# Two more expert blocks in seven-product form, and the last block's slot scatters issued together

## The chip, the cores and the metric

The kernel runs on one core of a Trainium2 chip. The metric is the device time of one execution in microseconds (us); the time before is the median of ten runs. All arithmetic is float32.

## The reference, cut to what matters

One causal self-attention layer over 4096 rows of 256, with a residual, and then a mixture of experts with a residual. The second half is where the change lies:

```python
h = layernorm(x) @ W_in + b_in                       # 4096 tokens x 256
probs = softmax(h @ W_gate + b_gate)                 # 8 experts
topv, topi = top_k(probs, 2); topv /= topv.sum()     # each token goes to two experts
mid  = relu(einsum('nd,edh->neh', h, W1) + b1)       # 256 -> 1024
eout = einsum('neh,ehd->ned', mid, W2) + b2          # 1024 -> 256
out  = x + einsum('ne,ned->nd', route, eout) @ W_out + b_out
```

The kernel computes only the two chosen experts of each token.

## The kernel before, in words

**Attention and routing.** Rows are worked in eight blocks of 512 tokens. While attention runs over them, each finished block is routed: every token gets a slot in the list of each of its two experts. A slot is written into the DRAM table `slots` by an indirect DMA on GpSimd (POOL), one for each 128 tokens and each of the two choices, so eight for each block. `put_tile` (L472, L473) is one such scatter: a copy of the 128 addresses to integers, and then the DMA. Scatters that are ready wait in the list `puts`; `put_one` takes one from it and pins it to the place where it is called, so that they are spread between other work.

**Items.** The tokens' slots are then worked as a list `work` of items. Items named `a` and `b` are blocks of 256 slots of one expert; `c`, `d` and `e` are smaller ones of one to four experts; `z` comes last and takes the slots that were left out. The first nine entries (0 to 8) are `a` items, entry 9 is the only `e` item, and entries 10 and 11 are `a` items again. For each item an expert's W1 and W2 are loaded (SyncE, SP), the tokens' rows are gathered (L1146, POOL), turned so that features lie on partitions (`rows_todo`: 32x32 transposes on VectorE (DVE), 16 for a pair of items), multiplied by W1 into `mid` (tiles `pm`), multiplied by W2 (`contribute`, tiles `pe`), and scattered to `parts` (L1531, POOL).

**Stages.** The loop `for n, item in enumerate(work)` runs as stages. Stage n computes `mid` of item n+2 and contributes item n. In the usual form `mid` takes 16 products of 128x256, each followed by an activation on ScalarE (ACT).

**Seven products.** Items for which `seven_of` holds take another form, `hidden_seven`: W1 and the tokens are each cut into a 2x2 matrix of blocks, and seven products take the place of eight, for each of four pairs of feature tiles. That makes 28 products of 128x128. It needs:

- `key_forms` (L1409 to L1412), at the end of stage n for item n+4: four sums of W1's quarters, 128x512 each, on POOL. One of them overwrites a quarter of W1 in place.
- `row_forms` (L1420 to L1423), inside the contribution of stage n for item n+3: four sums of the turned rows' quarters (tile `t`), 128x128 each, on POOL.
- In `hidden_seven` PE does products 0, 4, 1, then 5, 2, then 6 of all four pairs, with some units of item n's contribution between them. DVE then combines each pair (L1473, L1475), and only after L1475 of a pair may PE add product 3 into the same bank. Up to seven of the 16 units of the contribution lie ahead of those last four products, and nine behind them.

Before, the condition is `AHEAD + 3 < n` with `AHEAD = 3`. So items 7, 8, 11 and thirteen later ones have the form, 16 in all.

**Planning.** The last block's tokens (block 7) are entered in stage 0, and their places are counted in stage 1 by `counting()`, which appends eight scatters to `puts`. In stage 1 `plan_late` picks the slots of item `z`, and in stage 2 `plan` is called four times (tables `b`, `c`, `d`, `e`; L983 to L1020). Both are long chains of very small DVE instructions. From stage 3 on items depend on them: SP first runs `take_late` (L1076, L1077), which reads and clears slots and so waits for all scatters, and then fetches the slots of the `e` item and its successors (L1125) by the tables' addresses. `assert not puts` stands at the beginning of stage 3.

**Order.** Instructions given to `tc.keep_in_program_order` (in the loop by `pin`, from stage 3 on) keep the order in which they are written. The others, the sums of `key_forms`, the transposes of `turn_pair` and the planning among them, are placed by a scheduler when the program is built. After that each engine runs its own list strictly in order, waiting at each instruction for the semaphores of others. `fetch_pair` and `turn_pair` gather and turn two items at a time: 5 and 6, 7 and 8, 9 and 10.

Where the scatters of `puts` are taken in this loop:

```python
            if f % 2:
                put_one(nc.scalar.copy)      # hidden_units: four in each usual mid
...
            pin(nc.vector.tensor_tensor(y[:, u, :], pe[:, :D], c2, ALU.add))
            ease()
            put_one()                        # contribute_units: two in each 256-slot item
```

Of the kernel before, what the change touches and what calls it, by code (L numbers as in the profile page):

```python
# [57 lines left out]
SEVEN = True  # L58
# [5 lines left out]
def preln_attention_moe_kernel(  # L64
# [18 lines left out]
    nc = tc.nc  # L83
# [44 lines left out]
    def ps_o(name):  # L128
        return psum.tile([P, TB], F32, tag="o", name=name, bufs=3)
# [14 lines left out]
    def mul(*a, **k):  # L144
        done = nc.tensor.matmul(*a, **k)  # L145
        if ordered:
            tc.keep_in_program_order(done)
        return done
# [318 lines left out]
    puts = []  # L467
# [18 lines left out]
    def put_one(by=nc.vector.tensor_copy):  # L486

        if puts:
            tc.keep_in_program_order(puts.pop(0)(by=by))
# [592 lines left out]
    AHEAD = 3  # L1082
    FOUR = AHEAD + 6
    ALONE = FOUR + 2
    ALONG = (FOUR + 1,)
# [6 lines left out]
    work, blocks_work = blocks_work[:ALONE], blocks_work[ALONE:]  # L1092
# [300 lines left out]
        return [mid[:, f, :] for f in range(NF)], [partial(finish, f) for f in range(NF)]  # L1393

    def seven_of(n):
        return SEVEN and AHEAD + 3 < n < len(work) and work[n][0] in "ab" and n not in ALONG

    def key_forms(item, got):

# [493 lines left out]
    for n, item in enumerate(work):  # L1893
# [36 lines left out]
        if seven_of(n + 3):  # L1930

            def form(m):
                settle(m - 3.5)
                formed[m].append(row_forms(work[m], hTs[m]))

            forming.append(partial(form, n + 3))
# [6 lines left out]
        if coming + 1 < len(work) and seven_of(coming):  # L1943
            hTs.pop(coming)
            points = pieces + 2
            others = contribute_units(item, got.pop(n), mids.pop(n))
            mids[coming], behind[-coming] = hidden_seven(
                work[coming], got[coming], formed.pop(coming), others, ready
            )
        elif coming + 1 < len(work):  # L1950
            points = pieces + 2
            if "e" in (work[coming][0], work[coming - 1][0]):
                for do in ready:
                    do()
                ready = ()
                contribute(item, got.pop(n), mids.pop(n))
                send_second(upto2[n] + VT)
            mids[coming], behind[coming] = hidden(
                work[coming], got[coming], hTs.pop(coming), ready, False
            )  # L1960
        else:
            points = pieces
            for do in ready:
                do()
# [5 lines left out]
            turn_pair(AHEAD + 2)  # L1970
        if n == 1:
            counting()
        if n == 2:
            pn = ps_o("pnb")
            mul(pn[:, :NE], lhsT=ones, rhs=seen, start=True, stop=True)
            seen = const.tile([P, NE], F32, tag="sums", name="sums")
            nc.vector.tensor_copy(seen, pn[:, :NE])
            tables["b"] = plan("b", seen, NBLK - NFULL, SB, SEI - 1, tables["a"][2])

            def twice(k):  # L1980
                taken = const.tile([P, NE], F32, tag="twice" + k, name="twice" + k)
                nc.vector.tensor_scalar_mul(taken, tables[k][2], 2.0)
                return taken

            tables["c"] = plan("c", seen, NHALF, SH, SEI - 1, twice("b"))
            tables["d"] = plan("d", seen, 2 * NPAIR, SQR, SEI - 1, twice("c"))
            tables["e"] = plan("e", seen, NE, SEI, SEI - 1, twice("d"))
            tables["f"] = tables["e"]

            over = const.tile([P, 1], I32, tag="over", name="over")  # L1990
            nc.vector.tensor_scalar_add(over, tables["d"][3], float(4 - 2 * USUAL))
            nc.vector.tensor_tensor(over, over, tables["e"][3], ALU.max)
# [11 lines left out]
        if seven_of(n + 4):  # L2004
            formed[n + 4] = [key_forms(work[n + 4], got[n + 4])]
# [56 lines left out]
```

## Time and profile before

| | |
|---|---|
| median of ten runs | 1041.98 us (1039.56 to 1042.56) |
| the profiled execution | 1043.04 us |
| its span, first to last instruction | 1041.3 us |
| TensorE (PE) busy | 1032.6 us, 99% |
| DVE, ACT, POOL busy | 706.6, 406.9, 362.0 us |
| mean granted PE clock | 0.998 |
| DMA | 173.59 MB, mean 167 GB/s |

The span is the time between the first and the last instruction; 1.74 us of the execution lie outside it. Times of rows are counted from the span's start. The stages that matter here lie between 572 us (stage 0) and 667 us (the end of stage 6). A matmul of float32 shows as two records, so the 16 products of a usual `mid` are 32 records.

### The profile page before, as it was taken

The numbers are of one execution on the slowest core, as the hardware profiler recorded it, in microseconds if no ns is written. First come the engines' busy times: TensorE is split into PE (matmuls) and PEld (weight loads), VectorE is DVE, ScalarE is ACT, GpSimd is POOL, SyncE is SP. The second block draws the span as 40 slices with busy tenths as digits, with TensorE's granted clock in tenths as the row PEclk, the third lists the DMA queues.
The fourth block names the chain that finished last, engine by engine and source line by source line (L and its number), as shares of the span: only waits on it lengthen the run. The fifth ranks groups of instructions, "written<-read, shape, count | busy, mean of one in ns | idle before, by whom it ended". The sixth has DMA issues, their size and how long they took to land. (4 is left out here: it accounts for less than half of the span.)

```text
span 1041.3 us, 18934 instructions
## 1 busy us (share of the span) xinstructions
PE 1032.6 (99%) x6153; PEld 900.7 (86%) x6153; DVE 706.6 (68%) x2131; ACT 406.9 (39%) x1001; POOL 362.0 (35%) x439
## 2 busy tenths in 40 slices
PE   9999999999999999999999999999999999999998
PEld 7877889989989989999998887888798987889887
DVE  5765668766858777668797683487577675874346
ACT  2442344434425243424333222333443534436254
POOL 2201332212312120222024564354766466457110
PEclk9999999999999999999999999999999999999999
DMA  6433311121121110104455937799999989997685
GB/s 210 135 79 83 78 42 39 49 62 23 42 42 18 46 40 4 44 3 112 113 172 186 329 109 218 234 314 347 353 345 306 312 291 314 325 319 216 210 318 187
DMA packets 194891, 173.59 MB, mean 167 GB/s; under 512 B 82942, under 2 KB 169922, under 8 KB 194788
## 3 DMA queue, kind: packets, MB, share of 16 engines
q1 hardware_dynamic: 185956, 154.36, 47.9%
q0 software_dynamic: 8288, 17.45, 4.9%
q8 instruction: 50, 0.82, 0.3%
q10 hardware_dynamic: 544, 0.52, 0.1%
q14 instruction: 53, 0.43, 0.1%
HBM read 135.15 MB, written 30.44 MB: 159 GB/s over the span
## 5 line engine op out<-in xcount | busy, mean ns | idle before, releaser
L145 PE MATMUL ps<-qT,zT 128*128 128x256 f32 x1088 | 239.9, 373 | 0.8 <-DVE mx L690 0.8
L145 PEld LDWEIGHTS ps<-qT,zT 128*128 128x128 f32 x1088 | 200.8, 190 | 29.3 <-issue 2.2
L145 PE MATMUL po<-v,s 128*128 128x128 f32 (+1 forms) x672 | 125.8, 320 | 0.0
L145 PE MATMUL pe_a<-w_a,mid_a 128*128 128x256 f32 x544 | 124.9, 384 | 0.0
L145 PEld LDWEIGHTS pe_a<-w_a,mid_a 128*128 128x128 f32 x544 | 102.3, 192 | 15.5 <-issue 2.5
L145 PEld LDWEIGHTS po<-v,s 128*128 128x128 f32 x672 | 107.3, 191 | 9.1
L473 POOL DMA_INDIRECT slots<-assign,ati x64 | 63.6, 994 | 147.3 <-DVE ati L472 99.4
L684 ACT COPY s<-ps 128x512 f32<-128x512 f32 x120 | 69.4, 581 | 104.7 <-PE ps L145 99.5
L1292 DVE STREAM_TRANSPOSE hT<-h 32x192 f32<-32x192 f32 x240 | 88.7, 370 | 24.6 <-DMA h<-rows,slot_a 18.0
L787 ACT ACTIVATE s<-s 128x512 f32<-128x512 f32 x120 | 73.0, 629 | 72.7 <-DVE s L784 55.8
L690 DVE TENSOR_TENSOR mx<-ps,mx 128x512 f32<-128x512 f32 x91 | 62.5, 687 | 57.0 <-ACT s L684 56.1
L784 DVE TENSOR_TENSOR s<-s,pmax 128x512 f32<-128x512 f32 x120 | 77.1, 677 | 9.5 <-PE pmax L151 9.3
L145 PE MATMUL po<-v,sf 128*128 128x129 f32 x384 | 74.6, 276 | 0.1
L145 PE MATMUL pm_a<-hT,w_a 128*128 128x256 f32 (+1 forms) x304 | 59.0, 331 | 0.0
L145 PEld LDWEIGHTS po<-v,sf 128*128 128x128 f32 x384 | 58.3, 192 | 0.5 <-DVE sf L823 0.5
L145 PEld LDWEIGHTS pm_a<-hT,w_a 128*128 128x128 f32 x304 | 50.5, 191 | 5.5 <-issue 1.2
L1335 ACT ACTIVATE mid_a<-pm_a,c_a 128x256 f32<-128x256 f32 x64 | 30.3, 474 | 60.4 <-PE pm_a L145 53.7
L145 PE MATMUL pe_b<-w_b,mid_b 128*128 128x256 f32 x224 | 51.7, 380 | 0.1
L1531 POOL DMA_INDIRECT parts<-y_a,slot_a x34 | 34.0, 999 | 50.8 <-DVE y_a L1528 33.8
L1292 DVE STREAM_TRANSPOSE mid_d<-raw_d 32x256 f32<-32x256 f32 x96 | 41.8, 436 | 5.8 <-ACT raw_d L1371 4.3
L145 PEld LDWEIGHTS pe_b<-w_b,mid_b 128*128 128x128 f32 x224 | 41.1, 190 | 5.3 <-issue 0.5
L322 POOL TENSOR_SCALAR ln0rstd<-ln0mv 128x4 f32<-128x4 f32 (+1 forms) x9 | 2.2, 245 | 120.8 <-DVE ln0mv L316 120.2
(388 smaller groups left out, 1997.9 us busy)
## 6 DMA issues: line engine op xcount, KB each, us to landing
w_a<-in_L_ffn_W_dram SPq DMA_DIRECT2D x68, 512.0 KB, 6.1
w_d<-in_L_ffn_W_dram SPq DMA_DIRECT2D x48, 512.0 KB, 7.5
w_c<-in_L_ffn_W_dram SPq DMA_DIRECT2D x32, 512.0 KB, 7.8
w_b<-in_L_ffn_W_dram SPq DMA_DIRECT2D x28, 512.0 KB, 5.6
rows<-hr SPq DMA_DIRECT2D x16, 512.0 KB, 5.0
w_e<-in_L_ffn_W_dram SPq DMA_DIRECT2D x16, 512.0 KB, 5.1
yp<-parts SPq DMA_DIRECT2D x14, 512.0 KB, 7.4
after<-x SPq DMA_DIRECT2D x8, 512.0 KB, 2.9
```

Source lines behind the costliest of these rows:

```text
L145: done = nc.tensor.matmul(*a, **k)
L322: keep(nc.gpsimd.tensor_scalar_add(rstd[:, s, 0], mv[:, s, 1], EPS))
L473: put = nc.gpsimd.indirect_dma_start(out=slots, out_offset=bass.IndirectOffsetOnAxis(ap=ati, axis=0), in_=assign[:, TOPK * (b * TPB + j) + ...
L684: nc.scalar.copy(flat, ps)
L690: done = nc.vector.tensor_tensor(r.mx, ps, old, ALU.max)
L784: nc.vector.tensor_tensor(s, s, pm[:, :QB].unsqueeze(1).to_broadcast([P, KU, QB]), ALU.subtract)
L787: nc.scalar.activation(s, s, AF.Exp)
L1292: pin(easy.pop(0)[1]())
L1335: nc.scalar.activation(mid[f // 2][:, f % 2, :size], pm[:, :size], AF.Relu, bias=c1[:, f : f + 1])
L1531: put = nc.gpsimd.indirect_dma_start(out=parts, out_offset=bass.IndirectOffsetOnAxis(ap=slot[:, u : u + 1], axis=0), in_=y[:, u, :], in_of ...
```

## The change

Two conditions. `seven_of` begins two items earlier, so items 5 and 6 take the form of seven products too: 18 in all. And right after `counting()` in stage 1 all eight scatters of block 7 are issued one behind the other, with their address copies on ACT; before, one copy stood behind each output of items 1 and 2 (on DVE) and one behind every second activation of item 4 (on ACT).

```diff
     def seven_of(n):
-        return SEVEN and AHEAD + 3 < n < len(work) and work[n][0] in "ab" and n not in ALONG
+        return SEVEN and AHEAD + 1 < n < len(work) and work[n][0] in "ab" and n not in ALONG
...
         if n == 1:
             counting()
+            while puts:
+                put_one(nc.scalar.copy)
```

The functions that it calls (`key_forms`, `row_forms`, `hidden_seven`, `put_tile`) are unchanged.

## The prediction

> **What bounds the kernel now.** The page first: PE is busy for 1032.6 of 1041.3 us. Time can therefore only come from fewer products or from PE's own waits.
>
> ```profile
> PE 1032.6 (99%) x6153; PEld 900.7 (86%) x6153; DVE 706.6 (68%) x2131; ACT 406.9 (39%) x1001; POOL 362.0 (35%) x439
> ```
>
> Next, who waited for whom, on PE over the whole span. One entry leads, and it is in the seven-product form: product 3 waits for DVE's second combine.
>
> ```profile
> PE pm_a L145 <- DVE mid_a L1475: 2.1, 4, 1.5
> ```
>
> The timeline of PE (start, length, instruction, records, idle time before it) shows a usual `mid` at 607.30, then item 7's stage (5) up to 653.49, and item 8's.
>
> ```profile
> 607.30 7.07 PE L145 MATMUL pm_a<-hT,w_a 128*128 128x256 f32 x32
> ...
> 641.25 2.76 PE L145 MATMUL pe_a<-w_a,mid_a 128*128 128x256 f32 x12
> 645.51 0.46 PE L145 MATMUL pm_a<-t_a,w_a 128*128 128x128 f32 x2 [1.50 <-DVE mid_a L1475]
> ...
> 647.92 5.74 PE L145 MATMUL pe_a<-w_a,mid_a 128*128 128x256 f32 x18
> 653.49 0.38 PE L145 MATMUL pm_a<-hT,w_a 128*128 128x128 f32 x2
> ...
> 661.87 1.05 PE L145 MATMUL pm_a<-t_a,w_a 128*128 128x128 f32 x8
> ```
>
> Stage 5 lasts from 634.92 to 653.49, 18.57 us. Stage 6, the same work undisturbed, takes 13.13 us. So item 7 loses 5.44 us, more than the 2.1 us of the list of waits. Its four last products take 2.41 us (645.51 to 647.92) and not 0.89, since DVE needs 0.72 for each pair. And the 18 records behind them take 5.57 us where they should take 18 x 0.216 = 3.9. The busy times by stretch say why (last three columns: granted PE clock, DMA share, GB/s): after the gap the clock is half for some 3.5 us.
>
> ```profile
> 644.00:645.50 1.50, 0.01 (x1) 0.02 (x1) 1.33 (x5) 0.00 (x0) 1.20 (x2) 1.00 0.72 218
> ...
> 649.00:650.00 1.00, 1.00 (x4) 0.79 (x3) 0.95 (x3) 0.00 (x0) 0.92 (x4) 0.50 1.01 367
> ...
> 651.50:652.00 0.50, 0.50 (x4) 0.40 (x3) 0.00 (x0) 0.00 (x0) 0.25 (x1) 1.00 1.06 402
> ```
>
> Why DVE was late, from its timeline: it stood 18 us for gathered rows, turned ten tiles of the pair 9/10, and only then came to the combines at 644.54. Before that the planning ran from 604.14 to 620.13, and some of its tiny steps took 1 to 2 us in place of 0.16.
>
> ```profile
> 604.14 0.17 DVE L1977 COPY sums<-pnb 128x8 f32<-128x8 f32 x1
> ...
> 611.45 1.93 DVE L1019 CAST whose_id<-whosed 128x16 int32<-128x16 f32 x1
> ...
> 613.50 1.24 DVE L1982 TENSOR_SCALAR twiced<-nowd 128x8 f32<-128x8 f32 x1
> ...
> 619.96 0.17 DVE L1020 CAST base_ie<-basee 128x8 int32<-128x8 f32 x1
> ...
> 639.76 2.66 DVE L1292 STREAM_TRANSPOSE hT<-h 32x192 f32<-32x192 f32 x7 [18.03 <-DMA h<-rows,slot_a]
> ...
> 644.54 0.29 DVE L1473 TENSOR_TENSOR mid_a<-pm_a,mid_a 128x128 f32<-128x128 f32 x1
> ```
>
> POOL's timeline gives the partner: its four key sums stand at 612.06 to 617.19, and the slow DVE steps end with them. SP's shows where the rows came from: it waited for the last scatter until 620.78.
>
> ```profile
> 577.77 1.00 POOL L1531 DMA_INDIRECT parts<-y_a,slot_a  x1 [0.30 <-issue]
> ...
> 612.06 1.28 POOL L1409 TENSOR_TENSOR s_a<-w_a,w_a 128x512 f32<-128x512 f32 x1
> ...
> 632.78 0.94 POOL L1146 DMA_INDIRECT h<-rows,slot_a  x1 [0.30 <-issue]
> ```
>
> ```profile
> 620.78 0.59 SPq L1076 DMA_DIRECT2D late_slot<-slots  x1
> ...
> 625.23 2.81 SPq L1125 DMA_DIRECT2D slot_e<-slots  x4
> ```
>
> **Part 1, the products.** A usual stage is 13.81 us (607.30 to 621.11), one with seven products 13.13. Two items save 2 x 0.68 = 1.4 us.
>
> **Part 2, the scatters.** The eight still cost 8 x 1.27 = 10.2 us of POOL. In the order of the changed program they stand in one piece ahead of both outputs of item 1, so the last is out near 604 and not at 618.66. SP's wait until 620.78 falls away; its reads by table `e` then start when the planning ends, at P + 0.6, not at 625.23. The eight copies on ACT (0.18 each) lie in its idle time before 594.33. In the changed order three of the ten transposes stand ahead of item 6's combines and the other seven between those and item 7's, a whole stage earlier than needed, so item 7's 5.4 us go.
>
> **Part 3, POOL's queue.** The scheduler put the key sums of items 5 and 6 far ahead: three in front of the second four scatters of block 6, five in front of item 0's output and the four gathers of pair 7/8. Eight times 1.28 is 10.2 us for everything queued behind, the gathers and block 7's scatters. W1 of item 5 is issued at 563.74 and 565.01 and lands 6.5 later (median). So: three sums from 570 to 571.5, four scatters (5.1), the other five sums (6.4), item 0's output (now 577.77) at 585 to 587, gathers until 591 to 593, block 7's scatters and item 1's outputs until 605 to 607, and then the row sums of item 5. PE wants the first of these at 607.5. I take no wait; 1 us at most.
>
> **Part 4, DVE for item 5.** The combines of item 5 stand right behind the planning's last step. Call its end P. The pair 7/8 lands 1 to 3 us later than DVE now takes it (594.81), less the 1.0 us that POOL's key sums cost DVE there: sums start at 604.3 to 606. The planning takes 15.99 us now, 4.6 of which are four steps at 5.23 us in all instead of 0.64. Uncontended from 604.3 it ends at 615.7, and with the row sums of item 5 (four of 0.41 to 0.48) in its way at 616.5. But behind item 2's output, some 4 us before the end, POOL starts the key sums of item 7, the row sums of item 6 and, soon, the rest: about 7 us of sums against a dozen small steps. If these are slowed as now, P is 619 to 621. I take 619.5, near the 620.13 of now.
>
> A DVE instruction with two SBUF inputs, or in a two-port mode, is fully blocked while a GpSimd instruction that reads SBUF runs, says the Trainium skill (SBUF — State Buffer, Who interferes with whom). It speaks against this change, which adds 16 such sums; the 1.93 us row agrees. By it alone, with whoever issues first winning, P could be anything from 616.5 to 621.
>
> PE reaches product 3 of item 5 at 607.30 + 8.38 = 615.7 (8.38 as in stage 6, 653.49 to 661.87). It gets it 0.97 after DVE is free (644.54 to 645.51): 620.5. That is a wait of 4.8, then 1.5 of pacing (2.41 less 0.89), then 1.7 of half clock: 8.0 us. Bounds: P of 616.5 gives 1.8 + 1.5 = 3.3 without a clock drop; P of 621 gives 9.5.
>
> The gate closes after an idle window of about 3.4 us, says the skill (TensorE: Matmul & The Clock Gate, What's actually happening). Here 2.2 us of gaps within 4 us were enough. By the rule the low bound stays 3.3, by the row it would be 5.0; at P = 619.5 both give 8.0.
>
> **Part 5, a new wait for item 6.** In the changed order three transposes of pair 9/10 stand ahead of item 6's combines. Their rows landed at 639.76, 7.0 after the last gather was issued. The gathers now follow item 3's output and POOL's sums: last issue near 628.5 in place of 632.78, landed at 634 to 636; three transposes (0.38 each) and 0.97 make 636 to 638. PE wants it at 607.30 + 13.13 + 8.0 + 8.38 = 636.8. I take 1.2 with some pacing; 0 to 2.7. With a small wait at item 5 it is larger, 2 to 5, as the rows don't come earlier in proportion.
>
> **Sum.** -1.4 - 5.4 + 8.0 + 1.2 = +2.4 us. The profiled execution (1043.04) becomes 1045.4; it lies 1.06 above the median, so the median 1041.98 becomes 1044.4.
>
> **Rivals.** (a) *The wait only moves*, from item 7 to 5 and 6, at the same price: P near 617.5, waits of 5 to 8 together, net -2 to +1.5, about 1042. For it: DVE's steps slip in between POOL's sums, and 0.41 us row sums hold less than 1.28 us ones. (b) *Faster*: the rows of pair 9/10 come with slot reads 5 us earlier and DVE is through its planning by 616, so that PE waits about 1 at item 5 (with pacing 2.5) and 1 at item 6: -6.8 + 3.5 = -3.3, about 1038.7. It decides where P is under 616.5 and the rows land before 631. Against it: the bounds of part 4, and POOL's sums end near 622 whatever DVE does, so that gathers can hardly start before 624. (c) *POOL late as well*: item 5's row sums come after 608.5, which adds a wait on them and pushes all behind: +5, about 1047. That the form isn't taken at all is excluded by the order of the changed program.
>
> **How the numbers follow.** Forecast 0.60, (a) 0.18, (b) 0.15, (c) 0.07. A measurement of this kernel can tell about 0.2%, 2.1 us, from no change. The forecast's own range, with P from 618 to 621 and item 6's bounds, is 1041.7 to 1047.4; most of it is over +2.1, so of its 0.60 I put 0.42 slower and 0.18 the same. Of (a) 0.15 is the same and 0.03 slower. Slower is 0.42 + 0.03 + 0.07 = 0.52, same 0.18 + 0.15 = 0.33, faster 0.15. The range leaves out the end of (b) and the worst of (c): 1039.8 to 1047.6.
>
> **What would show it.** Right: in the list of waits, PE for L1475 in stage 3 with a gap of 3 to 6 us, half clock behind it, the last planning step at 618 to 621, no wait at item 7, and stages 3 to 5 together some 2.4 us over the present 46.19 (607.30 to 653.49). Wrong: planning done by 616, item 5's products unbroken, or stages 3 to 5 under 44 us; or a wait of PE for `t` of item 5; or PE losing time after 667, which I cost at nothing because PE there has no wait now.

## The result, and the profile after

The changed kernel takes 1051.62 us (median, 1050.07 to 1054.32), the kernel before, beside it, 1041.84. The ratio is 1.0098, with a 95% interval of 1.0088 to 1.0108: slower by 9.8 us, where 2.4 were predicted. The profiled execution takes 1051.23 us (span 1049.5); the one before took 1043.04, 1.2 above its median, so that the two spans differ by 8.2 only.

PE is busy for 1031.9 us (1032.6 before), so the time went into waits. What is new is in the list of who waited for whom (PE, whole span: total, times, longest). It is the entry that led before, five times as large:

```profile
PE pm_a L145 <- DVE mid_a L1475: 11.1, 5, 9.6
```

The timeline of PE, from item 5's stage (3) to item 7's (5):

```profile
612.71 2.76 PE L145 MATMUL pe_a<-w_a,mid_a 128*128 128x256 f32 x12
625.11 2.88 PE L145 MATMUL pm_a<-t_a,w_a 128*128 128x128 f32 x8 [9.63 <-DVE mid_a L1475]
627.78 5.09 PE L145 MATMUL pe_a<-w_a,mid_a 128*128 128x256 f32 x18
632.71 0.38 PE L145 MATMUL pm_a<-hT,w_a 128*128 128x128 f32 x2
...
642.03 0.46 PE L145 MATMUL pm_a<-t_a,w_a 128*128 128x128 f32 x2 [0.78 <-DVE mid_a L1475]
...
656.71 1.05 PE L145 MATMUL pm_a<-t_a,w_a 128*128 128x128 f32 x8
```

Stage 3 runs from 606.92 to 632.71, 25.79 us where the same work undisturbed takes 13.13. Stage 4 lasts until 648.33 (15.62), stage 5 until 661.49 (13.16): item 7's four last products are one unbroken row at 656.71, its loss is gone. Stages 3 to 5 together take 54.57 us; before it was 46.19. That is +8.38, which is the difference of the spans (8.2) within 0.2.

DVE's timeline shows why item 5 waits. The planning starts at 605.38. From 615.58 on three tiny steps take 7.19 us; steps of their kind and size take 0.16 to 0.21 each in the same planning, some 0.5 together. The first combine of item 5 stands right behind the planning's last step:

```profile
605.38 0.17 DVE L1979 COPY sums<-pnb 128x8 f32<-128x8 f32 x1
...
615.58 2.25 DVE L1020 CAST base_id<-based 128x16 int32<-128x16 f32 x1
...
617.82 3.68 DVE L1000 TENSOR_TENSOR starte<-starte,twiced 128x8 f32<-128x8 f32 x1
...
621.63 1.26 DVE L1009 TENSOR_TENSOR gride<-number,whosee 128x64 f32<-128x64 f32 x1
...
624.15 0.28 DVE L1473 TENSOR_TENSOR mid_a<-pm_a,mid_a 128x128 f32<-128x128 f32 x1
```

POOL's timeline has the partner of the longest step. That step of DVE is held from 617.82 until 621.50, through the end of one row sum and four further sums, and ends as L1410 does (621.47):

```profile
617.73 0.48 POOL L1422 TENSOR_TENSOR t_a<-hT 128x128 f32<-128x128 f32 x1
618.18 0.44 POOL L1421 TENSOR_TENSOR t_a<-hT,t_a 128x128 f32<-128x128 f32 x1
618.59 1.25 POOL L1412 TENSOR_TENSOR w_a<-w_a 128x512 f32<-128x512 f32 x1
619.81 0.44 POOL L1423 TENSOR_TENSOR t_a<-hT,t_a 128x128 f32<-128x128 f32 x1
620.22 1.25 POOL L1410 TENSOR_TENSOR s_a<-s_a,w_a 128x512 f32<-128x512 f32 x1
```

The busy times by stretch (us, five engines, then the granted PE clock, DMA share, GB/s) show the clock at half behind the wait, and back at full speed during the next 18 records:

```profile
625.10:627.80 2.70, 2.69 (x9) 2.09 (x10) 1.72 (x6) 1.10 (x3) 0.00 (x0) 0.50 0.03 0
627.80:632.70 4.90, 4.90 (x19) 4.14 (x19) 0.42 (x1) 0.37 (x1) 2.51 (x3) 0.79 0.47 135
```

### The profile page after: what moved, and what is told of

Same layout as the page of the kernel before. It is cut to its first block, busy times and chain, and to the rows that moved or that the text cites. A ratio compares the mean times of both kernels' runs of the same rounds, so it can differ in the third digit from the quotient of the medians.

```text
span 1049.5 us, 19097 instructions
## 1 busy us (share of the span) xinstructions
PE 1031.9 (98%) x6201; PEld 901.5 (86%) x6201; DVE 712.9 (68%) x2143; ACT 412.7 (39%) x1029; POOL 375.0 (36%) x455
## 5 line engine op out<-in xcount | busy, mean ns | idle before, releaser
L145 PE MATMUL pm_a<-hT,w_a 128*128 128x128 f32 (+1 forms) x272 | 50.1, 313 | 0.0
L145 PEld LDWEIGHTS pm_a<-hT,w_a 128*128 128x128 f32 x272 | 42.8, 191 | 4.0 <-issue 1.2
L145 PEld LDWEIGHTS pe_b<-w_b,mid_b 128*128 128x128 f32 x224 | 41.1, 190 | 5.3 <-issue 0.5
L1335 ACT ACTIVATE mid_a<-pm_a,c_a 128x256 f32<-128x256 f32 x48 | 22.7, 473 | 38.6 <-PE pm_a L145 38.6
```

What stands on the lines that cost most here:

```text
L1335: nc.scalar.activation(mid[f // 2][:, f % 2, :size], pm[:, :size], AF.Relu, bias=c1[:, f : f + 1])
```

## The experiments

Theory T: POOL's key and row sums hold DVE's planning steps; the end of the planning, P, sets item 5's combines, and PE waits for them. Rival W: the long steps wait for something else. Rival S: the scatters in one piece are what costs.

The runs fell on different chips. Beside the runs e1 to e4, e6 to e9 and g1 to g4 the kernel before takes 1077.5, 1077.2 and 1072.6 us; beside f and h it takes 1043.35 and 1043.01, like in the first comparison. On the slower chips PE has waits that the first traces lack, above all in stages 1 and 2. In the changed kernel there (e6, list of PE's waits) the largest is for ACT, in item 4's usual `mid`:

```profile
PE pm_a L145 <- ACT mid_a L1335: 13.2, 1, 13.2
```

What ACT itself waits for in that place (20.9 us) the trace puts down to no instruction; that engines wait there for their next instructions, as the expectation of e6 has it, is not shown. A trace of the kernel before on such a chip was not obtained. The totals from there are therefore given, but little is read from them. Lengths of the planning and waits of PE for DVE are read from these traces all the same, each inside one trace; but PE and DVE are late there by other amounts, so a wait at item 5 can be smaller for that reason alone. "Planning" is the time from the copy of the sums to the end of `base_ie`.

**The sums of item 6 and 7 moved behind the planning** (labels e3, e8, g3). In the changed kernel, where `put` is the output's scatter and `issue_after` orders POOL's queue (at both places it is item 3's first output):

```diff
+            parts_put[0] = put
...
-                formed[m].append(row_forms(work[m], hTs[m]))
+                if m == 6:
+                    with tc.issue_after(parts_put[0].ins):
+                        formed[m].append(row_forms(work[m], hTs[m]))
...
-            formed[n + 4] = [key_forms(work[n + 4], got[n + 4])]
+            if n == 3:
+                with tc.issue_after(parts_put[0].ins):
+                    formed[n + 4] = [key_forms(work[n + 4], got[n + 4])]
```

> The changed kernel, with one difference: the row sums of item 6 and the key sums of item 7 on POOL may begin only after item 3's first output, and so after the planning; POOL has nothing beside the planning's last steps. Theory T: the three steps that took 2.25, 3.68 and 1.26 us take some 0.5 together, the planning ends near 617.4 in place of 624.15, PE's wait at item 5 is about 3 us in place of 9.63, and stage 3 lasts 17 to 19.5 us in place of 25.79; the gathers of pair 9/10 come some 6 us earlier; what item 6 and 7 lose to their later sums on POOL is 0 to 3 us. The time is 1042 to 1047. Rival W (the three steps waited for something else, their own data for instance): they stay as long, and the time stays at 1050 to 1053.

> The changed kernel with the row sums of item 6 and the key sums of item 7 behind item 3's first output. Theory T: as in the run on the other chip, the planning takes 11 to 11.5 us from the copy of the sums to its last step, in place of 18.9; PE's wait at item 5 is 2 to 4 us in place of 9.6, the rows of pair 9/10 land earlier by about as much as the planning is shorter. 0.2 to 0.5 per cent over the kernel before, 0.5 to 0.8 per cent under the changed one. Rival W (the steps waited for something else): as slow as the changed kernel.

> The changed kernel with the row sums of item 6 and the key sums of item 7 behind item 3's first output, on such a chip. Theory T: the planning takes 11.1 us, or 12.5 where the row sums of item 5 fall into it; PE waits 2 to 3.5 us at item 5 with the pacing of 1.5 behind it, stage 3 lasts 16.5 to 19.5 us in place of 25.79. 0.1 to 0.5 per cent over the kernel before. Rival W (the slow steps have another cause): as the changed kernel, 1.0 per cent over.

Measured: 1.0100 [1.0070, 1.0130], 1.0094 [1.0068, 1.0119] and 1.0082 [1.0067, 1.0096] of the kernel before. The planning takes 11.04, 11.06 and 11.04 us, against 18.86 in the changed kernel of the first comparison and 14.97 in the one run on such a chip (e6). DVE's timeline of the third run, with the combine now waiting for PE:

```profile
626.47 0.17 DVE L1986 COPY sums<-pnb 128x8 f32<-128x8 f32 x1 [1.47 <-PE pnb L145]
...
637.34 0.17 DVE L1020 CAST base_ie<-basee 128x8 int32<-128x8 f32 x1
638.60 0.29 DVE L1473 TENSOR_TENSOR mid_a<-pm_a,mid_a 128x128 f32<-128x128 f32 x1 [1.08 <-PE pm_a L145]
```

So W falls: with the sums moved away the steps take their usual time. Stage 3 takes 13.16 in all three, with no wait at item 5. That is not due to the moved sums alone: PE was 13 us late by its wait for ACT in stage 2. With the start of the first comparison, 605.38, a planning of 11.04 would leave a wait of some 2 us (an estimate: 605.38 + 11.04 + 0.97 against 615.30, where PE wants product 3), and more with item 5's row sums in it. The expected gain in time did not come. One reason is that there was little to gain on such a chip: the changed kernel itself waits only 0.48 at item 5 there (e6). The other is visible in PE's timeline of the third run: item 6's row sums now stand behind the gathers on POOL, and PE waits for `t` of item 6.

```profile
650.97 0.49 PE L145 MATMUL pm_a<-t_a,s_a 128*128 128x128 f32 x2 [4.15 <-POOL t_a L1420]
```

Stage 4 takes 19.1 to 19.7 instead of 13.13, so item 6 loses some 6 us. The expectation had 0 to 3 us for items 6 and 7 together.

**Only item 7's key sums moved** (f1): the last hunk alone, and the line that records `put`.

```diff
-            formed[n + 4] = [key_forms(work[n + 4], got[n + 4])]
+            if n == 3:
+                with tc.issue_after(parts_put[0].ins):
+                    formed[n + 4] = [key_forms(work[n + 4], got[n + 4])]
...
```

> The changed kernel with only the four key sums of item 7 moved behind item 3's first output; the four row sums of item 6 stay beside the planning. Theory T: the planning, 11.05 us without any sums and 18.7 with all eight, comes to 12 to 13 us, since four row sums of 0.41 to 0.48 can hold DVE for no more than some 1.8 us in all. So the key sums are worth 5.5 to 6.5 of the 7.7 us. Rival (the row sums, between which DVE gets no turn either, hold as much as the key sums): 15 us.

Measured, one execution: 1046.7, beside 1043.35 for the kernel before. The planning takes 14.30 us, more than expected: two sets of row sums stand beside it, item 5's at its beginning as well as item 6's. Taken apart, the 7.82 us that the changed kernel's planning takes over 11.04 are 4.56 for four key sums and 3.26 for eight row sums. The rival's reading, that row sums hold DVE as key sums do, fits nearly as well for each microsecond: the eight fill 3.63 us of POOL. PE's wait at item 5 shrinks accordingly (timeline of PE):

```profile
619.66 0.46 PE L145 MATMUL pm_a<-t_a,w_a 128*128 128x128 f32 x2 [3.76 <-DVE mid_a L1475]
```

Stage 3 takes 19.81 in place of 25.79, stage 4 16.29. T holds on a chip without the other waits: P is 5.44 us earlier (618.71 against 624.15), the wait 5.87 shorter.

**The kernel before with item 8's key sums moved** (f2), neither half of the change:

```diff
-            formed[n + 4] = [key_forms(work[n + 4], got[n + 4])]
+            if n == 4:
+                with tc.issue_after(parts_put[0].ins):
+                    formed[n + 4] = [key_forms(work[n + 4], got[n + 4])]
...
```

> The kernel before with one edit: the four key sums of item 8 on POOL behind item 3's first output, and so after the planning. Theory T: the planning takes 11.0 to 11.5 us in place of 16.0, its last step comes 4.5 to 5 us earlier; the last scatter and the reads of slots come earlier as well, and item 7 loses 0 to 3 us in place of 5.4. 0.2 to 0.5 per cent faster than before, without either half of the change. Rival W (the slow steps are due to something else): planning and time unchanged.

Measured: 0.9960 [0.9944, 0.9976], faster. The planning takes 11.12 us in place of 15.99, the slots are read from 621.00 and not 625.23, the rows of pair 9/10 are there at 635.37 and not 639.76, and stage 5 takes 13.16 in place of 18.57. The same four sums, now late, make PE wait 1.87 for `t` of item 8 in stage 6. So POOL's sums cost the kernel before as well.

**The scatters alone** (e1, e7, g1, h2): `seven_of` as before, all eight scatters together.

```diff
-        return SEVEN and AHEAD + 1 < n < len(work) and work[n][0] in "ab" and n not in ALONG
+        return SEVEN and AHEAD + 3 < n < len(work) and work[n][0] in "ab" and n not in ALONG
```

> Only the second half of the change: the eight scatters together, items 5 and 6 in the usual form as before. Theory T (the loss of the changed kernel is the wait of item 5's seven products for DVE, whose planning is held up by POOL's sums): no seven-product item stands in stages 3 and 4, so PE waits at neither; the reads of slots start behind the planning's last step (about 620.5) and not at 625.23, so the rows of pair 9/10 land some 4 to 5 us earlier than 639.76 and the 5.4 us of item 7 go in part or whole. Stages 3 to 5 take 41 to 45 us where they took 46.19, the time is 1037 to 1041 us, faster than before. Rival S (the scatters in one piece are what costs: they hold up POOL's gathers and sums, and DVE with them): slower than before, 1044 us or more.

> Only the second half of the change: the eight scatters together, items 5 and 6 in the usual form as before. Theory T: PE waits in neither of stages 3 and 4; the reads of slots start behind the planning's last step and not after it by 5 us, the rows of pair 9/10 land some 4 to 5 us earlier against stage 5, and item 7's loss of 5.4 us goes. 0.1 to 0.5 per cent faster than before. Rival S (the scatters in one piece are what costs): slower than before by 0.2 per cent or more.

> Only the second half of the change (the eight scatters together, items 5 and 6 in the usual form), on a chip where the kernel before takes about 1042 us. Theory T: the planning is 16.0 us long, since the key sums of item 8 stand beside it; no wait at items 5 and 6; slot reads at once behind the planning, rows of pair 9/10 in time for item 7, whose 5.4 us go: 0.3 to 0.6 per cent under the kernel before. Rival S (the scatters in one piece are what costs): slower than before.

> The eight scatters together, items 5 and 6 in the usual form. On a chip where the kernel before takes about 1042 us theory T expects 0.3 to 0.6 per cent less than before, item 7 without a wait; rival S (the scatters in one piece cost) more than before. On a chip where it takes 1072 to 1077, 0.3 to 0.45 per cent more, as in the three runs there.

Measured on the three slower chips: 1.0045 [1.0025, 1.0066], 1.0028 [1.0008, 1.0048], 1.0038 [1.0026, 1.0051], slower than before, against T's number. Stages 3 and 4 are undisturbed (13.81 each), but stages 1 and 2 take 19 to 24 us each where they take 14 on the other chips. On the chip of h2: 0.9971 [0.9961, 0.9982], faster, as T says. There the planning takes 16.13, the slots are read at 619.55, and stage 5 takes 14.75; what is left of its loss is a wait for item 7's row sums on POOL (timeline of PE), no longer for DVE:

```profile
636.38 0.49 PE L145 MATMUL pm_a<-t_a,s_a 128*128 128x128 f32 x2 [1.32 <-POOL t_a L1420]
```

S falls for a chip like that of the first comparison. On the slower chips it does not: stages 1 and 2 together take 41.1 to 44.9 us in the ten traces with the scatters together, with items 5 and 6 in either form, and 35.1 and 35.3 in the two with the scatters spread (e2, g2, below; each shares its chip with traces of the first kind), where the wait for ACT in item 4's `mid` is also shorter than in e6 (e2, list of PE's waits):

```profile
PE pm_a L145 <- ACT mid_a L1335: 4.6, 1, 4.6
```

On the faster chips the two stages take 28.5 us with the scatters together (h2) or spread (f0). What makes ACT wait on the slower ones, and whether the copies on ACT have to do with it, is not shown.

**The seven products alone** (e2, g2), against the changed kernel:

```diff
             counting()
-            while puts:
-                put_one(nc.scalar.copy)
```

> Only the first half: items 5 and 6 in the form of seven products, the scatters spread over the outputs as before. Theory T: item 5's combines still stand behind the planning, and the same key and row sums still run on POOL beside its last steps, so PE waits 6 to 10 us at item 5 in stage 3; 1049 to 1054 us. Rival S (the scatters in one piece are what costs): near the kernel before, under 1045 us.

> Only the first half (items 5 and 6 with seven products, the scatters spread), on such a chip. Theory T: planning 18 to 19 us, stage 3 of 24 to 27 us, as in the changed kernel or worse by the scatters that stand between POOL's work; 0.8 to 1.4 per cent over the kernel before. Rival S: near the kernel before.

Measured: 1.0012 [0.9993, 1.0031] and 1.0026 [1.0016, 1.0036]. In e2 the planning takes 18.63 us, as in the changed kernel, and PE waits 3.10 at item 5; the length belongs to the seven products and not to the scatters. The expected 6 to 10 us of wait and 0.8 per cent failed: PE was late itself in stage 2 (20.67 and 20.88 us), so less of the planning was left when it reached product 3. In g2 the planning takes 14.27, since it began earlier against POOL's sums; there item 5 does not wait for DVE, item 6 does (3.12 us, stage 4 takes 21.32). On a chip of the faster kind this half was not run alone.

**The changed kernel again** (e6), for the scale on such a chip:

> The changed kernel itself beside the others, so that they can be compared with it on one chip. Where the chip is like that of the first comparison: 1.0 per cent over the kernel before, planning 18.9 us long (from the copy of the sums to the last step), a wait of 9.6 us at item 5. On a chip where engines also wait for their next instructions (as the first four experiments showed it, with the kernel before at 1077.5), theory T expects the planning as long, since its slow steps come from POOL and not from code, and the wait at item 5 smaller by what PE is late itself.

Measured: 1.0075 [1.0048, 1.0102]. The planning takes 14.97, not 18.9: it starts later against POOL's sums, so that item 5's row sums lie ahead of it and only 5.43 us of the later sums in it. They cost 3.93, less for each microsecond than on the faster chips. The wait at item 5 is 0.48.

**Item 6 alone** (e4):

```diff
-        return SEVEN and AHEAD + 1 < n < len(work) and work[n][0] in "ab" and n not in ALONG
+        return SEVEN and AHEAD + 2 < n < len(work) and work[n][0] in "ab" and n not in ALONG
```

> The changed kernel with item 5 in the usual form: item 6 alone is added to the items with seven products, 17 in all. Theory T: no wait in stage 3, which takes some 13.8 us; PE wants product 3 of item 6 near 607.3 + 13.8 + 8.4 = 629.5, while the combines now stand behind three transposes of pair 9/10, whose rows land at 634 to 638. So the wait moves to item 6 and is 5 to 10 us; stage 4 lasts 20 to 25 us, item 7 loses little. 1043 to 1050 us. Rival W (item 5's place just behind the planning is all that costs): item 6 loses 2.5 us as in the changed kernel and the whole is under 1041 us.

Measured: 1.0075 [1.0047, 1.0103]. Stage 3 takes 13.81, stage 4 20.54. DVE's combines begin at 658.60, behind three transposes whose rows came at 657.09 after 13.2 us of waiting, and PE's timeline has the wait:

```profile
659.57 0.46 PE L145 MATMUL pm_a<-t_a,w_a 128*128 128x128 f32 x2 [2.65 <-DVE mid_a L1473]
```

The wait moved to item 6, and the stage lasts as long as expected (20 to 25). The wait itself is shorter than 5 to 10, since PE was late by 1.8 us of other waits and the four products behind are paced.

**Item 6 with its combines first** (e9, g4, h1): e4, and no transposes of pair 9/10 ahead of the combines of items 6 and 7.

```diff
-        ease()
+        if item not in (work[6], work[7]):
+            ease()
         for i in pairs:
             put(i, 0, xs_, start=True)
```

> The scatters together, item 5 in the usual form, item 6 with seven products (17 in all), and the combines of item 6 ahead of every transpose of pair 9/10. Theory T: nothing that PE needs stands behind the planning or behind late rows, so no wait at item 5, 6 or 7; one item saves 0.68, item 7's 5.4 go. Stages 3 to 5 take 40.1 us (13.81 + 13.13 + 13.13) in place of 46.19, and the time is 0.5 to 0.6 per cent under the kernel before, faster than both kernels. Rival W (the place of item 6 behind late rows was not what made it wait): item 6 loses 2 us or more again.

> The scatters together, item 5 usual, item 6 with seven products and its combines ahead of all transposes of pair 9/10 (17 in all), on such a chip. Theory T: stages 3 to 5 take 40.1 us (13.81 + 13.13 + 13.13) in place of 46.19, the time is 0.5 to 0.6 per cent under the kernel before, and so under both kernels. Rival W (the place behind late rows was not what made item 6 wait): item 6 loses 2 us or more.

> The scatters together, item 5 usual, item 6 with seven products and its combines ahead of all transposes of pair 9/10. On a chip where the kernel before takes about 1042 us theory T expects 0.5 to 0.6 per cent less than before, stages 3 to 5 at 40.1 us. On a chip where it takes 1072 to 1077, 0.3 to 0.6 per cent more, as in the two runs there, from stalls in stages 2 and 4 that come from neither DVE's planning nor the rows.

Measured on the slower chips: 1.0050 [1.0031, 1.0068] and 1.0043 [1.0027, 1.0060]; item 6's combines wait for PE there and no longer for rows (7.56 us in e9, until 653.43), and what stage 4 still loses (17.3 to 17.7 us in all) is waits of PE for ACT and for what the trace calls issue, with half clock behind them. On h1's chip: 1037.7 us, 0.9956 [0.9940, 0.9972], under both kernels and the lowest median of all, though not clear of f2's 1038.7. Stages 3 to 5 take 13.81, 13.16 and 13.21, 40.18 together; 40.1 was expected. DVE's timeline shows the order that does it: the combines wait for PE, and the rows come later without anyone behind them:

```profile
626.35 0.29 DVE L1474 TENSOR_TENSOR mid_a<-pm_a,mid_a 128x128 f32<-128x128 f32 x1 [4.50 <-PE pm_a L145]
...
635.75 1.51 DVE L1292 STREAM_TRANSPOSE hT<-h 32x192 f32<-32x192 f32 x4 [6.32 <-DMA h<-rows,slot_a]
```

**The kernel before beside the others** (f0, h3):

> The kernel before, unchanged, for its trace on the chip of the other experiments, so that stages and planning can be compared there. Theory T: the planning takes 16.0 us as in the first trace (four key sums of item 8 stand beside it there too), stages 3 and 4 are undisturbed at 13.8 us each, item 7 loses 4 to 6 us behind the rows of pair 9/10. What this chip is slower by (1077 in place of 1042) lies in waits that have nothing to do with the change.

> The kernel before, for its trace beside the two others on one chip. Where that chip is one of the slow ones, the stall of 13 us that every other kernel shows there in stages 1 and 2 should be smaller in this one, if the address copies on ACT or the scatters in one piece have to do with it, and as large if they have not.

Both, one execution each, fell on a chip of the faster kind: 1042.13 and 1042.26 us, planning 15.97 and 15.77, stage 5 18.25 and 18.28. Planning and stage repeat those of the first trace within 0.35 us. So the question about the slower chips' stall was not answered by them. The stall of 13 us is not in every other kernel there, as the expectation of h3 says: with the scatters spread it is 4.6 and 4.8.

## Why the prediction was wrong

The direction and the mechanism were right: slower, by PE waiting for L1475 in stage 3 behind a planning that POOL's sums hold. The size was not, and 6.0 us are missing in stages 3 to 5: 4.66 in stage 3 and 1.29 in stage 4. In stage 3 the wait was too small by one term, P.

| step of the prediction | predicted | measured |
|---|---|---|
| Part 1, two stages with seven products | -1.4 | not measured alone; in h1 one such stage takes 13.16, 0.65 under the usual 13.81 |
| Part 2, item 7's loss goes | -5.4 | -5.41 (18.57 to 13.16) |
| Part 2, last scatter, late slots, slot reads | 604; earlier; P + 0.6 | 603.1; 608.10 in place of 620.78; 624.81 (P + 0.66) |
| Part 3, item 5's row sums | no wait | none (605.69 to 607.57) |
| Part 4, sums copied | 604.3 to 606 | 605.38 |
| Part 4, planning with nothing beside it | 11.4 | 11.04 to 11.12 (g3, f2) |
| **Part 4, P** | **619.5 (616.5 to 621)** | **624.15** (the first combine's start) |
| Part 4, loss in stage 3 | 8.0 | 12.66 |
| Part 5, loss in stage 4 | 1.2 (0 to 2.7) | 2.49 |

**The failed step is the price of POOL's sums at the planning's end, in part 4.** The prediction counted "about 7 us of sums against a dozen small steps" and then let them cost 3, from 616.5 to 619.5; the only support that it names is that 619.5 lies near the old end. Its own row of the trace before said otherwise: 5.1 us of key sums had cost 4.6. At that rate the 6.7 us of sums (616.10 to 622.81) cost 6.0, and P is 622.5, or 623.6 with the start at 605.38 in place of 604.3. They cost 6.66. The runs f1 and f2 put the rate at 0.9 to 0.96: 4.56 us for 5.05 us of key sums (f1), 4.87 for 5.1 (f2), 3.26 for eight row sums that fill 3.63 (f1). It is no constant: it was 0.86 in h1 (4.87 for 5.69) and 0.72 in e6. The upper bound of 621 was wrong for the same reason: it leaves 4.5 us for 6.7 us of sums, no more than 5.1 us of them had cost before. Of the 4.65 us that P was late, some 3.6 are this price and 1.1 the later start; the other parts of the planning cancel.

P being 4.65 late, the rest follows by the prediction's own formula: product 3 may run 0.97 after P, at 625.12, and was wanted at 606.92 + 8.38 = 615.30. The formula holds where PE has no other waits in the stage: 9.8 us against 9.63 read, in f1 3.9 against 3.76. In e2 product 3 also starts 0.96 after P (640.39 after 639.43), but PE had lost some 1.2 us elsewhere in the stage, so 3.10 are read where the formula has 4.3.

Pacing and half clock, 3.2 predicted, came to 2.8: 1.78 for the four products (2.67 in place of 0.89) and 1.04 for the 18 records behind (4.93 in place of 3.89). The clock had already fallen during the long wait (0.50 from 622.00 to 625.10), so part of its half-speed time passed over the wait and the paced products.

Stage 4's 2.49 is 0.94 of wait and 1.52 of pacing. The gathers of pair 9/10 ended with an issue at 633.43, not 628.5. Both things that they stand behind hang on P: the slot reads (624.81), and on POOL item 3's output (629.58), which comes late because PE is late. PE came later too, so the miss is only 1.3. That the late rows ahead of the combines make item 6 wait is shown by e4, where the combines stand behind them and PE waits for DVE, against e9, g4 and h1, where they went ahead and PE does not. In h1 stage 4 takes 13.16; item 5 is in the usual form there too.

The 5.4 us of item 7 went as forecast, but not for the forecast reason alone. The rows were to land at 634 to 636; DVE took them at 639.91, no earlier than before (639.76). They were in time because item 7's stage began 13.4 us later (648.33 against 634.92).

Of the rivals, "POOL late as well" had a time nearest to the result (1047), but not by its mechanism: nobody waits for item 5's row sums. Rival (b)'s benefit exists, though not with item 5: h1 has the earlier rows and keeps PE away from the planning.

The Trainium skill (SBUF — State Buffer, Who interferes with whom) says that a DVE instruction with two SBUF inputs contends with a GpSimd instruction that reads SBUF, and that the one that issues second is fully blocked. The longest step, of this kind, agrees (3.68 us through the end of one sum and four more, 0.15 to 0.17 for others of its size), and so do f1 and f2. If DVE were blocked through every sum, the estimate from this page would be 6.7 us lost for the 6.7 us of sums, where 6.66 were measured; the prediction let it widen its range and did not use it as a price. In e6, with 3.93 lost for 5.43, it would be too much.

## What to carry to other kernels

Price contention per microsecond of the partner's work, from a row that the trace already has, and multiply by what the change adds; take the product as a range, since how the two queues fall against each other moves it (0.72 to 0.96 here). The end of a chain in the old trace is no bound for the new one. Before giving PE work that depends on an engine, look at what stands in that engine's queue in front of it: item 5 was put behind the longest chain of the stage, item 6 behind late rows, and taking the one out and moving the other ahead turned +1.0% into -0.4% on the faster chips. Work moved out of one engine's way waits for its turn elsewhere (late row sums cost PE 4.15 us), so follow both queues.

## What the runs showed of the hardware

DVE is not let in between all of POOL's instructions: one step of 0.16 us was held through the end of one sum and four further ones, while other steps got through at other joints of the same row of sums. What decides it is not shown.

PE's clock can fall after short gaps, none of them over 1.5 us, and two traces that hardly differ came out differently. In f1's stage 4 a wait of 1.45 and three gaps of 0.17, 0.24 and 0.24 (2.10 us) left the 18 records behind at 3.88 us, full clock; in the kernel before a wait of 1.50 with the same gaps (2.15 us) was followed by half clock and 5.57 us. Whether the sum of the gaps alone decides is not shown.

Chips differ by 3% on this kernel. The slower ones have waits of ACT, DVE and SP for which the trace names no instruction (in e6 up to 20.9, 11.8 and 7.1 us). A change worth 0.3 to 0.45% came out with the opposite sign there (scatters alone, and item 6 first), and the scatters together go with 6 to 10 us more in stages 1 and 2. So a gain of this size is known for one kind of chip only.
